# Softplus of a scan kernel as one table function over four tiles, and two subtractions moved from GpSimd to VectorE

## The chip, the cores and the metric

One Trainium2 chip, one of its cores. The metric is the device time of one execution in microseconds (us), the median of several runs. PE is TensorE, DVE is VectorE, ACT is ScalarE, POOL is GpSimd, SP is the engine that issues nearly all DMAs.

## The reference, cut to what matters

Four layers, each a state-space mixer over a batch of 64 images of 11 x 11 positions and 128 channels, then a feed-forward part (mixture of experts, two recurrent ones, one with spectral filters). The change lies in the mixer, which is the same in all four layers, with other weights. Per layer:

```python
xz = x @ in_proj_w.T
xc, z = split(xz, 2)                          # 256 channels each
xc = silu(conv1d(xc as (B, 256, 121), 3 taps) + conv_b)
t = xc.transpose(0, 2, 1)                     # 121 "channels" d, 256 places l
# for each of two directions k, from t:
dts, Bs, Cs = x_proj_w[k] applied to t        # 8, 16, 16 rows
delta = softplus(dt_proj_w[k] @ dts + dt_proj_b[k])
dA  = exp(delta[..., None] * A)               # 16 states n
dBu = delta[..., None] * Bs * t[..., None]
h   = scan over l of  h = dA * h + dBu
y_k = sum_n h * Cs + Ds[k] * t
y = y_0 + flip(y_1);  normalized, times gelu(z), projected back to 128 channels
```

All values are fp32. `dts` and `dt_proj_w` are folded into one matrix `w_dt` (121 x 121 and a bias row), so that the argument of Softplus is one matmul of `t`.

## The kernel before, in words

**Stages.** Each layer is a scan stage of some 1630 to 1645 us from its first to its last scan (`Conv.run`, L771) and a feed-forward stage. The batch of 64 is cut into eight chunks c of CB = 8 images. A chunk has two directions k, so there are 16 *sets* (c, k), numbered m = 2c + k. A set has 121 channels d, taken two at a time: 61 *steps* (`PAIRS`), so a chunk has 122 steps and a layer 976. The partitions of the scan are 16 states x 8 images = 128.

**One scan step g** (two channels, 512 columns):
- `rows` (L677): TensorE spreads delta's rows, stored in three bf16 parts that add up to the fp32 value, over the 128 partitions into `da` in PSUM, a ring of five buffers. It is issued three steps ahead.
- `exps` (L690): ScalarE takes the exponential in place, with the scale A of its channel, two instructions, also three steps ahead.
- `load_u` (L654): SP loads `ub`, delta times t for four channels (two steps), 512 KB, from DRAM, spread over the states. Seven buffers, issued 14 steps ahead; SP waits there until the buffer's old scans are done.
- `times_b` (L666): GpSimd multiplies `ub` by B in place, 1024 columns, issued five steps ahead.
- `scan` (L698): VectorE scans `da` (PSUM) and `ub` (SBUF) into `H` or `HX`.
- `by_c` (L719) on TensorE sums over the states, and `keep_y` collects the sums: a copy on ScalarE for k = 0 (L736), an addition on VectorE for k = 1 (L734).

**Work laid beside the scans.** While chunk c is scanned, the next chunk's inputs are made: `lead` (normalization, transposes, the convolution, Silu, L264), `steps` (delta, below), `aside` (B and C, and the term with Ds: `scaled` on ScalarE, L393, then `skip` on VectorE, L398); and the chunk before is finished: `tail`, whose `scales2` (two small functions on ScalarE, L187 and L188) is followed a step later by `scales3` on VectorE (L192). `gate` makes Gelu (L433). The place of each piece is written out by hand: `at(step, f)` puts a function into a dictionary by step, `lay` spreads a list over a range of steps, `lay_at` takes (step, function) pairs; `run` emits for each step the rows and exponentials of g + 3, the loads and products that are due, the scan, and then that step's pieces. Every engine runs its instructions in this order, and an instruction that waits holds up all behind it on its engine.

**Delta (`steps`, L283).** A set has four *tiles* of two images, 128 x 512. The set (0, 0) is made before any scan starts (`alone`), with scratch space in `H`; the other 15 sets of a layer lie beside scans. Each tile goes through:

1. `project` (L304): TensorE, the argument x into PSUM (`p`).
2. `parts` (L311): ScalarE, relu(x) and |x| into SBUF.
3. `e` (L314, L319): ScalarE, p = exp(-|x|), then w = p + 1 (when alone, the addition is VectorE's, L317).
4. `ln` (L323): ScalarE, ln(w).
5. `less` (L326), `delta` (L329, L330): VectorE, relu(x) + (ln(w) - ((w - 1) - p)). Each reads one operand from PSUM and one from SBUF.
6. `first` (L335): ScalarE, the first bf16 part, into `d[:, 0]`; `u` (L339): GpSimd, delta times t; `rest` (L343): GpSimd, delta less the first part; `second` (L346): ScalarE, the second part; `third` (L350): GpSimd, what is left, as bf16. When alone, `rest` and `third` are VectorE's.
7. `store` (L353, L354): two DMAs on SP, `d` to `dD` and `u` to `uD` in DRAM, from where `load_r` and `load_u` fetch them. `d` and `u` have two buffers each.

With start s, tile i begins at s + i * apart; its operations 1 to 5 and `first` follow one step apart, then `u` at 6 + late, `rest` at 7 + late, `second` at 8.5 + late, `third` at 8 + 2 late, `store` at 10 + 2 late. For chunks from the third on, in steps of the chunk beside which they lie: k = 0 starts at 49, k = 1 at 95, both with apart 11.6 and late 6.

**Tables.** ScalarE's functions come in table sets. `act_tables(nc, 6)` (L69) loads the set with the exponential and the logarithm; a load in front of a function that isn't in the loaded set is put there when the kernel is built. Silu and Gelu stand each between two loads.

## Time and profile before

| what | us |
|---|---|
| median of three runs (lowest, highest) | 8470.6 (8464.77, 8479.49) |
| profiled execution, from its first to its last instruction (the span) | 8458.2 |
| scan stages, first to last scan, four layers | 1644.7, 1638.9, 1642.5, 1628.9 |
| a steady chunk (layer 0, third), span | 208.3 |
| VectorE busy in it | 178.3 |
| GpSimd busy in it | 182.6 |
| ScalarE busy in it | 169.3 |

The profile is of one execution; of its time only the span is given. A group line gives source line, engine, operation, written tile and read tiles, shape, count, then total busy us, the mean ns of one, and after the second bar the engine's idle time just before these instructions with what ended it. A line of a timeline gives start, duration, engine, line, operation, tiles, and in brackets the idle time before it. A line of waits gives who waited for whom: total us, times, longest. Delta's own groups beside the scans, all 128 x 512 and 240 times, with mean ns: ScalarE L311 590 and 598, L314 593, L319 688, L323 627, L335 611, L346 609; VectorE L326 682, L329 682, L330 687; GpSimd L339 1280, L343 1163, L350 1161. At the start of a layer, on VectorE, L343 680 and L350 1105.

### The profile page before, as it was taken

Reading aid. Unit: us, or ns where it says so; the run is one execution under the profiler, and the core shown is the slowest. Engines: PE = TensorE matmul, PEld = TensorE weight load, DVE = VectorE, ACT = ScalarE, POOL = GpSimd, SP = SyncE. Lnnn points to the kernel's source line nnn. Section 1 sums busy time; section 2 is a strip of 40 time slices with the busy share of each in tenths; the row PEclk is TensorE's granted clock in tenths of the full one; section 3 lists DMA queues with packets and bytes.
Section 4 is the critical chain, followed back from the end, with each engine's and each line's share of the span. In section 5 each row is a group of like instructions: output and inputs, shape, how many; then the busy total and the mean of one; then the engine's idle time right before and its main releaser. Section 6 shows DMA issues by size and latency. Waiting matters only on the chain.

```text
span 8458.2 us, 209204 instructions
## 1 busy us (share of the span) xinstructions
PE 5994.4 (71%) x83374; PEld 3445.8 (41%) x83374; DVE 6141.0 (73%) x8636; ACT 5768.7 (68%) x12927; POOL 5832.5 (69%) x3139
## 2 busy tenths in 40 slices
PE   5676677676677767767677777666567776766999
PEld 3343343355344434344344444344333433433445
DVE  6888888854888888872788888882688888883211
ACT  6888888743888878862788788863688888873210
POOL 6888888921988888850888888870688888890000
PEclk7777777767777777776777777766777778778999
DMA  6888998946898899960899999981689888992111
GB/s 171 221 224 223 223 226 225 232 140 177 218 224 225 224 220 222 230 181 25 222 220 227 221 226 226 224 205 31 179 226 225 230 225 226 226 231 72 39 34 37
DMA packets 933130, 1603.70 MB, mean 190 GB/s; under 512 B 139912, under 2 KB 620514, under 8 KB 932151
## 3 DMA queue, kind: packets, MB, share of 16 engines
q1 hardware_dynamic: 930871, 1588.21, 74.6%
q8 instruction: 655, 10.73, 0.6%
q14 instruction: 324, 2.65, 0.1%
q10 hardware_dynamic: 1280, 2.10, 0.1%
HBM read 1299.53 MB, written 290.52 MB: 188 GB/s over the span
## 4 chain that ended last, share of the span: by engine, by line
PE 31%; ACT 20%; DMA 17%; DVE 14%; issue 8%; POOL 7%; SPq 1%; DVEq 0%; POOLq 0%; ACTq 0%
ACT da L690 7%; DVE H L698 5%; DMA ub<-uD 5%; POOL ub L666 5%; PE da L677 4%; PE yb L719 4%; PE pc L253 4%; DVE HX L698 3%; DMA ts<-sD 3%; PE pu L1306 3%; PE acc L1309 3%; PE out L1349 2%; DMA uD<-u 2%; PE pst L1193 2%; DMA R<-dD 2%
## 5 line engine op out<-in xcount | busy, mean ns | idle before, releaser
L666 POOL TENSOR_TENSOR ub<-ub,Bt 128x1024 f32<-128x1024 f32 (+1 forms) x1984 | 4564.0, 2317 | 731.8 <-DMA ub<-uD 526.1
L690 ACT ACTIVATE da<-da,A 128x255 f32<-128x255 f32 x7744 | 3389.6, 446 | 1094.7 <-PE da L677 918.7
L698 DVE TENSOR_TENSOR_SCAN H<-da,ub 128x512 f32<-128x512 f32 x2048 | 2391.8, 1205 | 93.6 <-POOL ub L666 42.0
L677 PE MATMUL da<-R,pick 120*128 120x255 bf16 x7744 | 1783.5, 324 | 938.0 <-DVE H L698 529.4
L698 DVE TENSOR_TENSOR_SCAN HX<-da,ub 128x512 f32<-128x512 f32 (+1 forms) x1856 | 2115.6, 1187 | 90.5 <-issue 52.4
L677 PEld LDWEIGHTS <-pick 120*128 120x128 bf16 x7744 | 599.6, 104 | 1638.3 <-issue 777.1
L719 PE MATMUL yb<-H,Cz 128*16 128x64 f32 x32768 | 867.6, 255 | 349.8 <-ACT yst L736 260.4
L719 PE MATMUL yb<-HX,Cz 128*16 128x64 f32 x32768 | 856.5, 246 | 209.9 <-ACT yst L736 102.5
L719 PEld LDWEIGHTS yb<-H,Cz 128*16 128x16 f32 x32768 | 604.5, 112 | 921.4 <-issue 520.1
L719 PEld LDWEIGHTS yb<-HX,Cz 128*16 128x16 f32 x32768 | 562.4, 110 | 680.7 <-issue 316.8
L734 DVE TENSOR_TENSOR yst<-yst,yb 128x512 f32<-128x512 f32 (+2 forms) x640 | 340.2, 548 | 272.7 <-PE yb L719 272.5
L253 PE MATMUL pc<-w_conv,xnT 128*121 128x256 f32 x1344 | 441.6, 426 | 55.2 <-ACT t L257 55.1
L174 POOL MEMSET t<- 128x2048 f32 x4 | 7.2, 1804 | 597.4 <-PE px L1200 416.3
L736 ACT COPY yst<-yb 128x512 f32<-128x512 f32 (+2 forms) x640 | 330.6, 543 | 109.3 <-DMA yD<-yst 43.1
L304 PE MATMUL pd<-t,w_dt 122*128 122x512 f32 x480 | 358.3, 839 | 54.6 <-ACT t L264 54.6
L339 POOL TENSOR_TENSOR u<-relu,t 128x512 f32<-128x512 f32 x240 | 307.2, 1280 | 22.7 <-DVE relu L330 22.6
L350 POOL TENSOR_TENSOR d<-relu,d 128x512 bf16<-128x512 f32 x240 | 278.6, 1161 | 54.1 <-ACT d L346 53.9
L1273 DVE COPY U<-pu 128x488 f32<-128x488 f32 x128 | 85.4, 667 | 283.4 <-PE pu L1306 283.4
L1275 ACT COPY U<-pu 128x488 f32<-128x488 f32 x128 | 72.9, 569 | 309.2 <-PE pu L1306 309.2
L343 POOL TENSOR_TENSOR relu<-relu,d 128x512 f32<-128x512 f32 x240 | 279.1, 1163 | 6.6
L253 PEld LDWEIGHTS pc<-w_conv,xnT 128*121 128x121 f32 x1344 | 233.7, 209 | 102.8 <-ACT t L257 81.6
L643 POOL TENSOR_TENSOR Cz<-Cp,own 128x512 f32<-128x512 f32 x256 | 274.4, 1072 | 0.0
(242 smaller groups left out, 7929.8 us busy)
## 6 DMA issues: line engine op xcount, KB each, us to landing
ub<-uD SPq DMA_DIRECT2D x1920, 512.0 KB
dD<-d SPq DMA_DIRECT2D x256, 384.0 KB
R<-dD SPq DMA_DIRECT2D x192, 420.0 KB
uD<-u SPq DMA_DIRECT2D x256, 256.0 KB
sD<-s SPq DMA_DIRECT2D x128, 256.0 KB
yD<-yst SPq DMA_DIRECT2D x512, 60.5 KB
ts<-sD SPq DMA_DIRECT2D x56, 512.0 KB
y<-yD SPq DMA_DIRECT2D x112, 242.0 KB
```

The source lines that it names most:

```text
L253: nc.tensor.matmul(pc, lhs, rhs, start=(j == 0), stop=(j == taps - 1))
L304: nc.tensor.matmul(s["p"], self.w_dt[:, k, :], tb[: D + 1], start=True, stop=True)
L339: nc.gpsimd.tensor_mul(s["u"], s["relu"], tb)
L343: less.tensor_sub(s["relu"], s["relu"], s["d"][:, 0, :])
L350: less.tensor_sub(s["d"][:, 2, :], s["relu"], s["d"][:, 1, :])
L666: self.nc.gpsimd.tensor_mul(x, x, self.bc[m, "Bt"].unsqueeze(1).to_broadcast([128, n, L]))
L677: self.nc.tensor.matmul(self.da[g % RING][:, j, 1:], self.pick[:n, d % 5].rearrange("p n b -> p (n b)"), self.R[m, d // 35][:n, d % 35 // ...
L690: self.nc.scalar.activation(x, x, AF.Exp, scale=self.A[:, m % 2, d : d + 1])
L698: self.nc.vector.tensor_tensor_scan(self.H[dq % 2][:, :n, p - DQ[dq][0]], self.da[g % RING].rearrange("p j l -> p (j l)")[:, :n], x.rearra ...
L719: self.nc.tensor.matmul(self.yb[32 * q : 32 * q + 16, slot % 8, :, :, :w], self.Cz[slot // 8][:, place % 64 : place % 64 + 2, :].rearrange ...
L734: nc.vector.tensor_add(dst, dst, src)
L736: nc.scalar.copy(dst, src)
```

## The change

Softplus becomes one table function. Beside the scans, ScalarE copies each of the four projections from PSUM into a 2048-column buffer `sp`; then one instruction takes Softplus of all four tiles in place, with a table load ahead of it (put there when the kernel is built) and an explicit load of set 6 behind it. `parts`, `e`, `ln`, `less` and `delta` are gone. In the set made alone, Softplus reads each projection from PSUM by itself, and set 6 is loaded once behind the last tile; the load of set 6 behind the first chunk's Silu is left out. `rest` and `third` are VectorE's everywhere; both operands of each are in SBUF. The constants of the plan change: from the third chunk on, k = 0 has its projections at steps 49, 51, 53, 55, each copied a step later, Softplus at 57, and tile i begins at 58 + 8.3 i with `u` and `first`; k = 1 has Softplus at 103 and tiles at 104 + 11.6 i. `rest`, `second`, `third`, `store` follow at late, late + 2, late + 4, late + 6. For the second chunk (laid beside the first) k = 0 has Softplus at 75, tiles 6 apart, late 4, and k = 1 starts at 103 with tiles 9.3 apart; the set (0, 1) has Softplus at 8, tiles 8 apart, late 3.

```diff
-        self.one = fixed.tile([128, 1], F32, name="one")
-        nc.vector.memset(self.one, 1.0)
...
-            if b1 == CB:
+            if b1 == CB and c > 0:
                 act_tables(nc, 6)
...
         alone = c == 0 and k == 0
+        v = {}
+
+        def soft():
+            nc.scalar.activation(v["sp"], v["sp"], AF.Softplus)
+            act_tables(nc, 6)
+
         for b in range(0, CB, 2):
...
-            def parts(s=s, tile=tile):
-                for n, f in (("relu", AF.Relu), ("abs", AF.Abs)):
-                    s[n] = tile(n)
-                    nc.scalar.activation(s[n], s["p"], f)
-
-            def e(s=s, tile=tile):
-                nc.scalar.activation(s["p"], s["abs"], AF.Exp, scale=-1.0)
-                s["w"] = tile("w")
+            def keep(b=b, s=s):
                 if alone:
-                    nc.vector.tensor_scalar_add(s["w"], s["p"], 1.0)
-                else:
-                    nc.scalar.activation(s["w"], s["p"], AF.Identity, bias=self.one)
-
-            def ln(s=s, tile=tile):
-                s["ln"] = tile("ln")
-                nc.scalar.activation(s["ln"], s["w"], AF.Ln)
-
-            def less(s=s):
-                nc.vector.scalar_tensor_tensor(s["p"], s["w"], -1.0, s["p"], ALU.add, ALU.subtract)
-
-            def delta(s=s):
-                nc.vector.tensor_sub(s["p"], s["ln"], s["p"])
-                nc.vector.tensor_add(s["relu"], s["relu"], s["p"])
-
+                    s["sp"] = self.spare[0][:, 256 * b : 256 * b + 512]
+                    nc.scalar.activation(s["sp"], s["p"], AF.Softplus)
+                    if b == CB - 2:
+                        act_tables(nc, 6)
+                    return
+                if b == 0:
+                    v["sp"] = work.tile([128, CB // 2 * 512], F32, name="sp", bufs=1)
+                s["sp"] = v["sp"][:, 256 * b : 256 * b + 512]
+                nc.scalar.copy(s["sp"], s["p"])
...
-                nc.scalar.copy(s["d"][:, 0, :], s["relu"])
+                nc.scalar.copy(s["d"][:, 0, :], s["sp"])
...
-                nc.gpsimd.tensor_mul(s["u"], s["relu"], tb)
+                nc.gpsimd.tensor_mul(s["u"], s["sp"], tb)
 
             def rest(s=s):
-                less = nc.vector if alone else nc.gpsimd
-                less.tensor_sub(s["relu"], s["relu"], s["d"][:, 0, :])
+                nc.vector.tensor_sub(s["sp"], s["sp"], s["d"][:, 0, :])
 
             def second(s=s):
-                nc.scalar.copy(s["d"][:, 1, :], s["relu"])
+                nc.scalar.copy(s["d"][:, 1, :], s["sp"])
 
             def third(s=s):
-                less = nc.vector if alone else nc.gpsimd
-                less.tensor_sub(s["d"][:, 2, :], s["relu"], s["d"][:, 1, :])
+                nc.vector.tensor_sub(s["d"][:, 2, :], s["sp"], s["d"][:, 1, :])
...
-            at = start + b // 2 * apart
-            for i, f in enumerate((project, parts, e, ln, less, delta, first)):
-                out.append((at + i, f))
-            at += 6
-            for i, f in ((late, u), (late + 1, rest), (late + 2.5, second), (2 * late + 2, third), (2 * late + 4, store)):
-                out.append((at + i, f))
+            if alone:
+                at = start + b // 2 * apart
+                out += [(at, project), (at + 1, keep)]
+                at += 2
+            else:
+                out += [(start + b, project), (start + b + 1, keep)]
+                at = start + CB + 1 + b // 2 * apart
+            offsets = (0, 0, 0, 1, 1, 2) if alone else (0, 0, late, late + 2, late + 4, late + 6)
+            out += [(at + i, f) for i, f in zip(offsets, (u, first, rest, second, third, store))]
+        if not alone:
+            out.append((start + CB, soft))
         return sorted(out, key=lambda x: x[0])
...
-        self.lay_at(self.steps(0, 1, 0, 8.5, 2))
+        self.lay_at(self.steps(0, 1, 0, 8, 3))
...
-                a, b, e, apart, late, f = (24, 42, 66, 8.3, 2, 101) if c == 0 else (0, 16, 48, 11.6, 6, 95)
+                a, b, e, apart, late, f = (24, 42, 66, 6, 4, 103) if c == 0 else (0, 16, 48, 8.3, 6, 95)
...
-                self.lay_at(self.steps(c + 1, 1, s + f, (139 - f) / 4 if c == 0 else 11.6, late))
+                self.lay_at(self.steps(c + 1, 1, s + f, 9.3 if c == 0 else 11.6, late))
```

More of the change, by code (lines that the diff above doesn't have):

```diff
@@ L290, in steps @@
             tb = self.t[:, b : b + 2, :].rearrange("p b l -> p (b l)")
-            def tile(n, b=b):
-                if alone:
-                    at = 1024 * b + 512 * ("relu", "abs", "w", "ln").index(n)
-                    return self.spare[0][:, at : at + 512]
-                tag, bufs = ("abs", 1) if n == "ln" else (n, 2 if n == "relu" else 1)
-                return work.tile([128, 512], F32, name=n, tag=tag, bufs=bufs)
             def project(b=b, s=s, tb=tb):
```

## The prediction

> **What bounds the kernel now.** I read the page's busy line, then stretches of one steady chunk (layer 0, third chunk, scan steps 70 to 105), then who waits on VectorE, then single instructions.
>
> ```profile
> PE 5994.4 (71%) x83374; PEld 3445.8 (41%) x83374; DVE 6141.0 (73%) x8636; ACT 5768.7 (68%) x12927; POOL 5832.5 (69%) x3139
> ...
> L666 POOL TENSOR_TENSOR ub<-ub,Bt 128x1024 f32<-128x1024 f32 (+1 forms) x1984 | 4564.0, 2317 | 731.8 <-DMA ub<-uD 526.1
> L690 ACT ACTIVATE da<-da,A 128x255 f32<-128x255 f32 x7744 | 3389.6, 446 | 1094.7 <-PE da L677 918.7
> L698 DVE TENSOR_TENSOR_SCAN H<-da,ub 128x512 f32<-128x512 f32 x2048 | 2391.8, 1205 | 93.6 <-POOL ub L666 42.0
> ```
>
> The shares of 68 to 73% are averages over four scan stages (about 6550 us) and four feed-forward stages. By stretch (VectorE is the third busy column, GpSimd the fifth, then clock, DMA share, GB/s):
>
> ```profile
> 548.60:587.00 38.40, 30.77 (x465) 18.41 (x464) 27.66 (x41) 28.86 (x63) 31.06 (x14) 0.83 1.01 266
> 587.00:618.90 31.90, 23.71 (x388) 15.96 (x389) 28.68 (x38) 28.72 (x69) 24.69 (x16) 0.62 0.79 176
> 618.90:684.80 65.90, 46.61 (x804) 23.78 (x805) 61.49 (x74) 55.40 (x127) 65.74 (x36) 0.79 0.89 238
> ```
>
> From 618.9 to 684.8 us, GpSimd is full (65.7 of 65.9), VectorE nearly so (61.5). Steps 30 to 50 (548.6 to 587.0) belong to the DMA (share 1.01). So no engine alone is the bound, and freeing GpSimd helps only as far as VectorE, the next in line, lets it. VectorE runs the scans in order, and every stall of it is a stall of the chain. In this chunk of 208.3 us it is busy 178.3 and idle 30. What its idle time waits for:
>
> ```profile
> DVE yst L734 <- PE yb L719: 272.5, 175, 4.8
> ...
> DVE pd L326 <- ACT w L319: 104.4, 95, 2.9
> DVE tr L192 <- ACT tr L188: 92.3, 34, 3.6
> DVE pd L329 <- ACT ln L323: 91.7, 72, 4.6
> ```
>
> GpSimd is hardly among its releasers (42 us at L698). So I cost the change on VectorE's time line.
>
> **What the skill says.** First, the Trainium skill, "SBUF — State Buffer", section "Who interferes with whom": a VectorE instruction with two SBUF inputs takes the port pair that it shares with GpSimd, and is shut out for as long as a GpSimd instruction reading SBUF runs, and the reverse; with one SBUF input it isn't. The trace agrees, in both directions, at the start of layer 0, where the two subtractions already run on VectorE:
>
> ```profile
> 49.20 0.68 DVE L343 TENSOR_TENSOR H<-H,d 128x512 f32<-128x512 f32 x1
> 49.43 1.61 POOL L339 TENSOR_TENSOR u<-H,t 128x512 f32<-128x512 f32 x1 [2.50 <-DVE H L330]
> ...
> 57.09 1.29 POOL L339 TENSOR_TENSOR u<-H,t 128x512 f32<-128x512 f32 x1 [6.05 <-DMA uD<-u]
> 57.39 1.53 DVE L350 TENSOR_TENSOR d<-H,d 128x512 bf16<-128x512 f32 x1 [1.48 <-ACT d L346]
> 58.85 0.68 DVE L343 TENSOR_TENSOR H<-H,d 128x512 f32<-128x512 f32 x1
> ```
>
> GpSimd's product takes 1.61 us instead of 1.29 behind a subtraction; the subtraction that finds it running takes 1.53 instead of 0.68: it ends 0.54 after the product (58.38). All other VectorE work around the scans, the scans too, has at most one input in SBUF. Second, "ScalarE: Activation LUTs", section "What ACT_TABLE_LOAD costs": 1283 ns a load, plus some 1380 of drain. The trace has the 1.28, but the next function starts at once (below), so I count no drain. Third, same page, "Step-by-step: what each stage is for": 0.833 ns an element whatever the function; here gelu over 1936 columns took 1.82 us (L433), so Softplus over 2048 is taken as 1.9.
>
> **The change, part by part.** A layer has 16 delta sets of four tiles; one runs alone before the scans. That leaves 60 sets, 240 tiles in the kernel. VectorE instructions of 0.69 us follow each other every 0.60 (48.60, 49.20, 49.81 at the start), so 0.60 is what one takes of the line.
>
> (1) Three VectorE operations per tile go (L326, L329, L330): 720 x 0.60 = -432 us.
>
> (2) Their waits for ScalarE go: 104.4 + 91.7 = -196 us. What is late next: the scan behind them, whose inputs were there (it waited 20 us for da).
>
> (3) Two subtractions per tile come: 480 x 0.60 = +288 us. The operations read at most one buffer that ScalarE wrote two steps (3.4 us) before, and u's product stands four or six steps ahead; no further wait.
>
> (4) The shared port. GpSimd was busy 182.6 of 208.3 us in the chunk; without 8 tiles x 2 x 1.16 (L343, L350) it is 164, so with a chunk of about 213 a subtraction finds it busy 0.77 of the time. What then remains of its instruction is half of it: half of 2.37 for the products with B (88% of its time), half of 1.1 to 1.3 for the rest, together 1.11; the example shows that 0.13 of that is covered by VectorE's own start. So 0.77 x 0.98 = 0.76 us each, 480 x 0.76 = +365 us. Queued behind it on VectorE is the next scan; TensorE's rows (a ring of five) and the loads of ub wait for that scan. Bounds: 0 (always finds it idle) and 0.98 each, 470 us.
>
> (5) Softplus between two loads: 1.28 + 1.9 + 1.28 = 4.5 us of ScalarE in one piece, 60 times. The nearest thing is the Silu block, with scales2 a step later:
>
> ```profile
> 580.94 1.28 ACT L264 ACT_TABLE_LOAD   x1
> 582.23 2.00 ACT L264 ACTIVATE t<-t 121x1024 f32<-121x1024 f32 x2
> 584.25 1.28 ACT L71 ACT_TABLE_LOAD   x1
> ...
> 586.93 0.16 DVE L192 SCALAR_TENSOR_TENSOR tr<-pk,tr 128x4 f32<-128x4 f32 x1 [3.65 <-ACT tr L188]
> ```
>
> Of 4.6 us of block, VectorE lost 3.65, although exponentials run three steps ahead. The new block at step 57 has the same neighbour: the tail's scales2 at 58 and scales3 on VectorE at 59. That at 103 has `scaled` at 103 and `skip` on VectorE at 104. In six chunks of each layer both occur: 48 x 3.65 = 175; the other 12 blocks have no such neighbour, 0.75 each: together +184 us. Bounds: 0 (the lead hides it) and 60 x 4.6 = 276.
>
> (6) The set before the scans, where everything waits for it: from the last Silu (37.40) to the last store (66.55) the kernel spends 29 us. New: load 38.7, Softplus 39.3, u 40.7 (rest overwrites what u reads), rest, second, third, store by 43.5; the next tiles follow some 3.5 us apart, each held by its d buffer's earlier store (2.9 us from 53.28 to 56.22), last store near 55. -11 us a layer, -44 us.
>
> (7) TensorE: the fourth projection (L304) of a set stood at step 83 amid the projections for B and C, where VectorE waited 3 us for yb (part of the 272.5). It moves to step 55, where TensorE has room: 24 x 1.3 = -30 us.
>
> (8) At nothing: ScalarE loses 743 us (relu 142, abs 144, exp 142, identity 165, ln 151) and gains 240 copies x 0.57 and 60 x 4.5, net -336, but isn't the bound; GpSimd's 558 us relief (some 180 given back to the port) likewise, since VectorE hardly waited for it. Stores (both DMAs of `store`, on SP's queue, with the loads of ub behind) move from steps 71 to 106 to 70 to 95, and by one step for k=1; nothing new waits there. The two d and u buffers come free 4.6 steps (7.7 us) after a store's issue; if that is late, ScalarE and GpSimd wait up to 2 us, with lead to cover it; without it, 24 x 2 tiles x 1 = 50 us.
>
> Sum: -432 - 196 + 288 + 365 + 184 - 44 - 30 = +135 us. The span 8458.2 becomes 8593; the median of 8470.6 stands 12.4 above the span (the page gives no other time), which I keep: 8606 us.
>
> **Rivals.** *A, the forecast*: VectorE is the line, the port decides; +135, own range 8500 to 8820. *B, faster*: VectorE comes to its subtraction when GpSimd has just finished. Where GpSimd sets the pace, a pair of scans (2.4) ends as a product (2.37) ends, so what remains would be near zero; with VectorE the pace-maker GpSimd stands waiting for ub loads (already 526 us). At 0.25 us each, (4) is 120, the sum -110: 8360. It decides below 0.76 - 135/480 = 0.48 us. For it: in stretch 548.6 to 587.0 GpSimd waits. Against: no subtraction falls in that stretch; they fall at steps 64 to 93 and 110 to 149. *C, no change*: the port wait is near 0.48, or half the blocks hide: 8470. *D, much slower*: GpSimd's instructions follow without a gap, and if a waiting subtraction isn't let in between, it waits for a further product: + 480 x 2.37 = 1138, 9740. No row shows VectorE waiting with a second product queued. *E, the edit does not do what it says*: if copies brought loads of their own, 240 x 1.28 on ScalarE; the copies beside Silu and Gelu show none.
>
> **How the numbers follow.** A 0.58, B 0.26, C 0.07, D 0.09, E negligible. About 0.2% (17 us) is what a measurement tells from no change here. Faster 0.26, same 0.07, slower 0.58 + 0.09 = 0.67. The range reaches up to (4) and (5) at their upper bounds: 135 + 105 + 92 + 20 = +352, 8825; down to the middle of B, 8375; left out are B's lower half and most of D.
>
> **What would show it.** (1), (2): L326 and L329 gone from VectorE's waits. (4): the subtractions on VectorE with a mean near 0.68 + 0.76 = 1.4 us; a mean under 1.1 means B, over 2.5 D. GpSimd's products grow slightly over 2.37. (5): ScalarE with 120 more table loads; VectorE's wait L192 for L188 about doubled, and a new one of `skip` for `scaled`. (6): the first scan 11 us earlier. I am wrong if the steady chunk isn't longer than 208 us although the subtractions take 1.4.

## The result, and the profile after

| | kernel before | changed kernel |
|---|---|---|
| median of four runs, us (lowest, highest) | 8467.69 (8464.61, 8479.49) | 8566.44 (8558.9, 8570.5) |
| span of the profiled execution, us | 8458.2 | 8561.2 |
| granted TensorE clock, mean | 0.778 | 0.77 |

The ratio is 1.0116, 95% interval 1.0102 to 1.0131: the change costs 98.8 us. The forecast was 8606 us, with 8500 to 8820 as the likeliest case's own range.

The page of the changed kernel, its busy line and the groups that the prediction spoke of (line, engine, operation, tiles and shape, count, then busy us, mean ns, and the idle time before with what ended it; lines are those of the changed kernel, 15 to 20 lower than before: L321 is `u`, L324 `rest`, L330 `third`, L651 the products, L675 the exponentials, L683 the scans):

```profile
PE 6088.2 (71%) x83374; PEld 3490.2 (41%) x83374; DVE 6254.9 (73%) x8328; ACT 5526.0 (65%) x12103; POOL 5460.7 (64%) x2659
...
L651 POOL TENSOR_TENSOR ub<-ub,Bt 128x1024 f32<-128x1024 f32 (+1 forms) x1984 | 4664.3, 2371 | 839.4 <-DMA ub<-uD 664.7
L675 ACT ACTIVATE da<-da,A 128x255 f32<-128x255 f32 x7744 | 3393.5, 446 | 1329.4 <-PE da L662 1160.0
L683 DVE TENSOR_TENSOR_SCAN H<-da,ub 128x512 f32<-128x512 f32 x2048 | 2392.0, 1205 | 111.5 <-POOL ub L651 61.0
...
L321 POOL TENSOR_TENSOR u<-sp,t 128x512 f32<-128x512 f32 x240 | 319.3, 1330 | 487.6 <-ACT sp L289 419.3
...
L324 DVE TENSOR_TENSOR sp<-sp,d 128x512 f32<-128x512 f32 x240 | 371.6, 1548 | 0.0
L330 DVE TENSOR_TENSOR d<-sp,d 128x512 bf16<-128x512 f32 x240 | 294.2, 1226 | 0.0
```

VectorE has 308 instructions fewer (8328 for 8636) and is busy 114 us longer. ScalarE and GpSimd are relieved, by 243 and 372 us, and the kernel is slower all the same. The two subtractions (L324, L330) take 1.55 and 1.23 us where the same shapes took 1.16 on GpSimd. The exponentials and the products wait more, for the rows and the loads. Rows and loads wait in turn for a buffer that a scan of VectorE has to free (rows for scans: 1003 us, 690 before), so I take these waits for a consequence, not for the cause.

By stretches, the third chunk of layer 0 again (steps 30 to 50, 50 to 70, 70 to 105; columns as in the prediction):

```profile
549.72:587.30 37.58, 31.35 (x464) 18.74 (x462) 27.61 (x42) 28.50 (x62) 29.71 (x14) 0.77 1.05 265
587.30:622.39 35.09, 24.56 (x449) 15.71 (x448) 27.61 (x34) 32.17 (x71) 24.77 (x14) 0.80 0.73 170
622.39:687.84 65.45, 42.08 (x684) 21.94 (x683) 58.00 (x65) 45.11 (x97) 54.76 (x28) 0.78 0.86 234
```

The prediction's third window, 618.9 to 684.8 us, is not steps 70 to 105, as it says: the scan of step 105 began at 677.98, and the window runs on to step 109. The same steps before:

```profile
618.94:677.98 59.04, 41.02 (x716) 21.57 (x715) 54.63 (x68) 49.66 (x115) 58.88 (x33) 0.78 0.87 235
```

The stretch bound by the DMA (share 1.05) is as long as before (37.6 for 38.4 us). The second, which now holds a Softplus block (step 57), is 3.2 us longer than before, with VectorE busy no longer than it was (27.6 for 28.7). The third is 6.4 us longer: VectorE is busy 3.4 us longer (58.0 for 54.6) and idle 3.0 us longer, and it is now the fullest engine, while GpSimd, full before (58.9 of 59.0), has gaps. Steps 0 to 30, where four projections, their functions and the waits behind them are gone, took 53.2 and now 46.9. The whole chunk: 208.3 before, 212.6 after.

The same over all layers, mean length of each chunk in us, from its first scan to the next chunk's, for the eighth to the end of its last scan:

| chunk | 1st | 2nd | 3rd | 4th | 5th | 6th | 7th | 8th |
|---|---|---|---|---|---|---|---|---|
| before | 205.7 | 207.0 | 208.9 | 209.7 | 208.4 | 209.4 | 208.6 | 181.7 |
| after | 219.6 | 214.8 | 214.5 | 212.3 | 211.8 | 212.0 | 211.4 | 176.6 |

Over the four layers the first chunks give +55 us, the second to seventh +99, the eighth, beside which no delta is made, -20, and the start of the layers -43: from the last Silu to the first scan it takes 31 to 33 us instead of 42 to 43 (in layer 0 the first scan begins at 69.58 us instead of 79.76). That is +91; the spans differ by 103, and the other 12 us lie between a layer's last scan and the next layer's last Silu, mostly in the feed-forward stages, which the change doesn't touch.

What VectorE waits for in the changed kernel (total us, times, longest):

```profile
DVE tr L190 <- ACT tr L186: 197.5, 59, 4.5
DVE yst L719 <- PE yb L704: 191.5, 127, 4.9
DVE y L453 <- PE pk L445: 166.1, 45, 6.9
...
DVE s L383 <- ACT ps L378: 118.5, 32, 6.2
...
DVE y L453 <- DMA y<-yD: 44.8, 12, 5.9
```

and in the kernel before, for two of them:

```profile
DVE y L468 <- PE pk L460: 48.1, 10, 6.3
...
DVE s L398 <- ACT ps L393: 5.8, 25, 1.4
```

The waits for Softplus's steps (196 us before) are gone. `scales3` for `scales2` (L190) went from 92.3 to 197.5, `skip` for `scaled` (L383) from 5.8 to 118.5, the tail's normalization for its transposes (L453 for pk) from 48.1 to 166.1; the wait for yb fell from 272.5 to 191.5, that for y's load from 90.5 to 44.8. In sum VectorE's idle time is 11 us less than before: nearly all that was saved in waits was given back in other waits. With 114 us more of busy time, that is the difference of the spans, 103 us.

The two mechanisms can be seen in single instructions. The port, beside the third chunk of layer 0 (start, duration, engine, line, operation; VectorE first, then GpSimd):

```profile
626.39 2.23 DVE L324 TENSOR_TENSOR sp<-sp,d 128x512 f32<-128x512 f32 x1
...
633.59 2.84 DVE L330 TENSOR_TENSOR d<-sp,d 128x512 bf16<-128x512 f32 x1
...
628.03 1.51 POOL L628 TENSOR_TENSOR Cz<-Cp,own 128x512 f32<-128x512 f32 x1
...
633.52 2.36 POOL L651 TENSOR_TENSOR ub<-ub,Bt 128x1024 f32<-128x1024 f32 x1
635.82 1.53 POOL L628 TENSOR_TENSOR Cz<-Cp,own 128x512 f32<-128x512 f32 x1
```

The second subtraction starts just behind a product (633.52 to 635.88) and takes 2.84 us: it ends at 636.43, 0.55 after the product. GpSimd's next instruction takes 1.53 instead of its usual 1.07 (the one at 628.03, behind the first subtraction, 1.51): it waits for the subtraction in turn, and so the subtraction was let in between two instructions that follow each other without a gap. So it was with all that waited: 317 of the 480 found GpSimd in the way, each ended 0.55 us after the GpSimd instruction that was then running, and behind 287 of them GpSimd's next one followed within 0.2 us. The longest of all 480 is 2.88 us. This is what the Trainium skill says in "SBUF — State Buffer", "Who interferes with whom": whichever starts first keeps the pair for its whole instruction, and the other one waits. Who comes next when GpSimd has a further instruction ready, the page doesn't say; the last section shows that being let in is not certain.

The block, at step 57 of the second chunk of layer 0, ScalarE:

```profile
390.06 1.28 ACT L289 ACT_TABLE_LOAD   x1
391.35 1.91 ACT L289 ACTIVATE sp<-sp 128x2048 f32<-128x2048 f32 x1
393.28 1.28 ACT L71 ACT_TABLE_LOAD   x1
394.58 0.93 ACT L675 ACTIVATE da<-da,A 128x255 f32<-128x255 f32 x2
```

For 4.5 us no exponential is taken. Beside it VectorE waits 4.46 us in front of L190, and GpSimd, whose product `u` (L321) stands right behind Softplus, waits 7.85:

```profile
396.47 0.16 DVE L190 SCALAR_TENSOR_TENSOR tr<-pk,tr 128x4 f32<-128x4 f32 x1 [4.46 <-ACT tr L186]
...
393.34 1.26 POOL L321 TENSOR_TENSOR u<-sp,t 128x512 f32<-128x512 f32 x1 [7.85 <-ACT sp L289]
```

### The profile page after: what moved, and what is told of

Read it like the earlier page. It is cut to its first block, busy times and chain, and to the rows that moved or that the text cites. A ratio compares the mean times of both kernels' runs of the same rounds, so it can differ in the third digit from the quotient of the medians.

```text
span 8561.2 us, 207075 instructions
## 1 busy us (share of the span) xinstructions
PE 6088.2 (71%) x83374; PEld 3490.2 (41%) x83374; DVE 6254.9 (73%) x8328; ACT 5526.0 (65%) x12103; POOL 5460.7 (64%) x2659
## 4 chain that ended last, share of the span: by engine, by line
PE 35%; ACT 20%; DVE 18%; DMA 13%; issue 9%; POOL 3%; SPq 1%; DVEq 0%; ACTq 0%; POOLq 0%
ACT da L675 7%; DVE H L683 7%; PE da L662 6%; PE yb L704 5%; DVE HX L683 4%; PE pc L251 4%; DMA ts<-sD 3%; DMA ub<-uD 3%; PE pd L301 3%; PE acc L1294 2%; PE out L1334 2%; PE pu L1291 2%; POOL ub L651 2%; PE pst L1178 2%; DMA bcD<-bc 2%
## 5 line engine op out<-in xcount | busy, mean ns | idle before, releaser
L651 POOL TENSOR_TENSOR ub<-ub,Bt 128x1024 f32<-128x1024 f32 (+1 forms) x1984 | 4664.3, 2371 | 839.4 <-DMA ub<-uD 664.7
L675 ACT ACTIVATE da<-da,A 128x255 f32<-128x255 f32 x7744 | 3393.5, 446 | 1329.4 <-PE da L662 1160.0
L683 DVE TENSOR_TENSOR_SCAN H<-da,ub 128x512 f32<-128x512 f32 x2048 | 2392.0, 1205 | 111.5 <-POOL ub L651 61.0
L683 DVE TENSOR_TENSOR_SCAN HX<-da,ub 128x512 f32<-128x512 f32 (+1 forms) x1856 | 2119.9, 1185 | 67.1 <-POOL Cz L628 19.0
L662 PEld LDWEIGHTS <-pick 120*128 120x128 bf16 x7744 | 624.6, 104 | 1738.0 <-issue 1199.0
L321 POOL TENSOR_TENSOR u<-sp,t 128x512 f32<-128x512 f32 x240 | 319.3, 1330 | 487.6 <-ACT sp L289 419.3
L301 PE MATMUL pd<-t,w_dt 122*128 122x512 f32 x480 | 323.3, 760 | 247.6 <-ACT sp L313 194.6
L719 DVE TENSOR_TENSOR yst<-yst,yb 128x512 f32<-128x512 f32 (+2 forms) x640 | 337.9, 544 | 192.9 <-PE yb L704 191.5
L324 DVE TENSOR_TENSOR sp<-sp,d 128x512 f32<-128x512 f32 x240 | 371.6, 1548 | 0.0
L499 PE MATMUL po<-out_wT,y 128*121 128x128 f32 x896 | 202.6, 366 | 154.1 <-DVE tr L190 103.8
L628 POOL TENSOR_TENSOR Cz<-Cp,own 128x512 f32<-128x512 f32 x256 | 306.9, 1199 | 0.0
L330 DVE TENSOR_TENSOR d<-sp,d 128x512 bf16<-128x512 f32 x240 | 294.2, 1226 | 0.0
```

The costliest lines, as they stand in the source:

```text
L301: nc.tensor.matmul(s["p"], self.w_dt[:, k, :], tb[: D + 1], start=True, stop=True)
L321: nc.gpsimd.tensor_mul(s["u"], s["sp"], tb)
L324: nc.vector.tensor_sub(s["sp"], s["sp"], s["d"][:, 0, :])
L628: self.nc.gpsimd.tensor_mul(self.Cz[u], C.unsqueeze(2).to_broadcast([128, 64, CB]), self.own.unsqueeze(1).to_broadcast([128, 64, CB]),)
L651: self.nc.gpsimd.tensor_mul(x, x, self.bc[m, "Bt"].unsqueeze(1).to_broadcast([128, n, L]))
L662: self.nc.tensor.matmul(self.da[g % RING][:, j, 1:], self.pick[:n, d % 5].rearrange("p n b -> p (n b)"), self.R[m, d // 35][:n, d % 35 // ...
```

## The experiments

Two accounts of the +98.8 us stood against each other. The *port account*: the subtractions beside GpSimd's products cost what decides. The *block account*: Softplus between its loads does. Each ratio below is to the kernel before, run on the same chip. The changed kernel was not run again beside them: its own ratio, to compare, is 1.0116 (1.0102 to 1.0131), and where a time of it is needed, it is 1.0116 times the kernel before on that chip, an estimate good to some 12 us.

### The subtractions back on GpSimd

```diff
-                nc.vector.tensor_sub(s["sp"], s["sp"], s["d"][:, 0, :])
+                less = nc.vector if alone else nc.gpsimd
+                less.tensor_sub(s["sp"], s["sp"], s["d"][:, 0, :])
```

and the same for `third`.

> The changed kernel with the two subtractions beside the scans back on GpSimd; Softplus as one function stays. Port theory: the subtractions cost VectorE 480 x (0.60 + 0.71) = 630 us of its line, so VectorE is relieved by that, GpSimd takes 558 us back and becomes the bound in the stretches where it was full before: 8350 to 8450 us, GpSimd idle in a steady chunk back to about 25 us, VectorE idle up to 40. Block theory (the 4.5 us pieces of ScalarE make the change slower, and the port waits fall into time that VectorE would have idled): within 30 us of the changed kernel, 8540 to 8600.

Measured: 8428.21 us, ratio 0.9981 (0.9971 to 0.999). Moving the 480 subtractions from VectorE to GpSimd turns a loss of 1.2% into a gain of 0.2%, as the port account expected (8350 to 8450 us): their place is enough to decide the sign. This run doesn't tell the port from the instructions themselves. And the gain is small for an engine that got 595 us of work less:

```profile
PE 6062.8 (72%) x83374; PEld 3458.4 (41%) x83374; DVE 5659.5 (67%) x7848; ACT 5494.7 (65%) x12103; POOL 5813.9 (69%) x3139
```

```profile
DVE yst L721 <- PE yb L706: 380.9, 201, 8.4
...
DVE HX L685 <- ACT da L677: 99.8, 75, 2.6
DVE HX L685 <- POOL ub L653: 95.4, 95, 3.3
DVE H L685 <- POOL ub L653: 87.5, 50, 14.9
```

VectorE's busy time falls from 6255 to 5660 us, and its idle time grows by 454: it now waits for TensorE's sums (381 for 192), and for exponentials and products (in the order of the lines 100, 95 and 87 us, for 18, 3 and 61 in the changed kernel). With the subtractions gone, VectorE is not the only bound any more.

### The old Softplus with the subtractions on VectorE

The kernel before, with only this edit:

```diff
-                less = nc.vector if alone else nc.gpsimd
+                less = nc.vector
```

in `rest` and in `third`.

> The kernel before with the two subtractions moved to VectorE, and nothing else of the change. Port theory: + 480 x (0.60 + 0.71) = 630 us on VectorE's line, a part of it back where GpSimd had been full: 8800 to 9050 us, mean of a subtraction 1.3 to 1.5 us. Block theory: 8440 to 8500, since GpSimd's relief pays for VectorE's load.

Measured: 8828.04 us, ratio 1.0457 (1.0437 to 1.0476), +384 us, inside the port account's range; the mean of the 480, 1.54 us, lies just above it. The two groups of this kernel:

```profile
L343 DVE TENSOR_TENSOR relu<-relu,d 128x512 f32<-128x512 f32 x240 | 405.7, 1690 | 2.6 <-POOL u L339 2.6
...
L350 DVE TENSOR_TENSOR d<-relu,d 128x512 bf16<-128x512 f32 x240 | 331.9, 1383 | 15.7 <-ACT d L346 15.7
```

The move alone costs 384 us; VectorE is busy 680 us longer, and its idle time falls by 312. Made in the kernel with the new Softplus, the same move costs 113 us (8428.21 to 1.0116 x 8443.6 = 8541.5). So the two edits don't add up. In the kernel before, more than half of the 680 us that VectorE got came out as time; in the kernel with the new Softplus, where VectorE is busy 595 us longer with the subtractions, a fifth did. There its idle time shrank by 454 us to take them in, for 312 here.

### The same VectorE instructions without the port

Beside the scans, an instruction with one SBUF input of the same size takes the place of each subtraction. The subtractions are left out, so the three parts no longer add up to delta:

```diff
-                nc.vector.tensor_sub(s["sp"], s["sp"], s["d"][:, 0, :])
+                if alone:
+                    nc.vector.tensor_sub(s["sp"], s["sp"], s["d"][:, 0, :])
+                else:
+                    nc.vector.reduce_max(s["sp"], s["sp"].unsqueeze(2), axis=AX.X)
```

and likewise for `third`.

> The changed kernel in which beside the scans each of the two subtractions is replaced by a maximum over one element, an instruction of VectorE of the same size with a single SBUF input; the subtraction is left out (the parts of delta no longer add up). Port theory: the mean of these 480 instructions falls from 1.39 to about 0.7 us, 330 us less on VectorE's line, time 8230 to 8330 us. Block theory: the time stays within 40 us of the changed kernel.

Measured: 8276.03 us, ratio 0.9805 (0.9783 to 0.9828). Its groups:

```profile
L327 DVE TENSOR_REDUCE sp<-sp 128x512 f32<-128x512 f32 x240 | 158.4, 660 | 0.0
L336 DVE TENSOR_REDUCE d<-sp 128x512 bf16<-128x512 f32 x240 | 158.5, 660 | 0.0
```

All 480 take 653 to 680 ns, beside the same products. VectorE is busy 338 us less than in the changed kernel, GpSimd 170 less, and the time is 265 us less (8541.5 to 8276.0). The instructions themselves aren't the price; what they wait for is. The edit also takes away that each subtraction needs ScalarE's copy just before it, but there was nothing to gain there: in the changed kernel VectorE's idle time in front of L324 and L330 is 0.0.

### Softplus without its loads

A function that is in set 6 takes the place of Softplus, which is left out, and the explicit load goes:

```diff
-            nc.scalar.activation(v["sp"], v["sp"], AF.Softplus)
-            act_tables(nc, 6)
+            nc.scalar.activation(v["sp"], v["sp"], AF.Exp)
```

> The changed kernel with an exponential in place of Softplus beside the scans and so without the 120 table loads: the block on ScalarE is 1.9 us instead of 4.5; Softplus is left out. Port theory: the 48 blocks with a neighbour that VectorE waits for lose 2.6 us each, 48 x 2.6 = 125 us: 8430 to 8480. Block theory: the whole of the loss and more comes back, 8330 to 8400.

Measured: 8315.0 us, ratio 0.9844 (0.9822 to 0.9866): 226 us less than the changed kernel, for 154 us less of ScalarE (120 loads of 1.283 us). The function took the same 1.91 us. So the loads cost 3.8 us of time a block for 2.6 us of ScalarE. The port account expected far less (8430 to 8480 us), and even the block account, nearer, less than this (8330 to 8400); of the two, this run speaks for the block. VectorE's waits in it:

```profile
DVE yst L718 <- PE yb L703: 145.7, 131, 5.3
DVE tr L190 <- ACT tr L186: 132.7, 62, 3.6
DVE y L452 <- PE pk L444: 132.7, 34, 6.0
```

The wait of L190 falls from 197.5 to 132.7, that of `skip` from 118.5 to 32.3, yb from 191.5 to 145.7, pk from 166.1 to 132.7. VectorE is busy as long as in the changed kernel (6251 for 6255): the 226 us are all waits. Little of it can come by way of GpSimd's `u`, whose wait for Softplus fell from 419 to 331 us only.

Both accounts are true, then: port 265, loads 226. They need not add, and no run takes both away.

### The blocks away from their neighbours

If the block costs because `scales3` and `skip` stand behind it, it should cost less elsewhere. From the third chunk on, two steps later for k = 0 and five for k = 1, whose tiles stand 11 apart for 11.6:

```diff
-                self.lay_at(self.steps(c + 1, 0, s + e + 1, apart, late))
-                self.lay_at(self.steps(c + 1, 1, s + f, 9.3 if c == 0 else 11.6, late))
+                self.lay_at(self.steps(c + 1, 0, s + e + (1 if c == 0 else 3), apart, late))
+                self.lay_at(self.steps(c + 1, 1, s + f + (0 if c == 0 else 5), 9.3 if c == 0 else 11, late))
```

> The changed kernel with the Softplus blocks of the third and later chunks moved away from the ScalarE instructions that VectorE waits for: k = 0 two steps later (Softplus at 59, behind scales2 at 58), k = 1 five steps later (at 108, behind the last `scaled` at 106), k = 1's tiles 11 apart. Theory of neighbours: the cost is in what stands right behind the block (scales3's and skip's waits, 105 and 103 us more than before, and TensorE's work held up behind them); 150 to 220 us come back, ratio to the kernel before 0.985 to 0.995. Theory of ScalarE's time: 4.5 us without an exponential starve the scans wherever they stand; at most 60 us come back, ratio 1.004 to 1.012, with new waits of the scans for da.

Measured: 8575.17 us, ratio 1.0151 (1.0132 to 1.0171): no gain, rather a loss. It lies outside what either account expected (0.985 to 0.995 for the neighbours, 1.004 to 1.012 for ScalarE's time). The neighbours' waits did fall (L190 from 197 to 141, `skip` from 118 to 28), but the scans themselves began to wait in their place:

```profile
DVE H L683 <- POOL u L321: 92.8, 24, 3.9
```

and the subtractions, which now met other instructions of GpSimd, took 1.49 us in the mean instead of 1.39. That is 48 us of VectorE, under which a small gain could lie hidden: this run alone doesn't decide. The same move with the subtractions on GpSimd, where VectorE doesn't wait for the port, tells more: it brought 0.9974 for 0.9981 (below), in a kernel in which GpSimd is fuller. My account by neighbours falls.

### The second chunk's tiles farther apart

The first chunk of a layer, beside which the second chunk's delta is made, lost most (+13.9 us), and in that of layer 0 GpSimd waited 10.9 us and ScalarE 7.3 us for the stores out of the two `u` and `d` buffers.

```diff
-                a, b, e, apart, late, f = (24, 42, 66, 6, 4, 103) if c == 0 else (0, 16, 48, 8.3, 6, 95)
+                a, b, e, apart, late, f = (24, 42, 66, 7, 3, 103) if c == 0 else (0, 16, 48, 8.3, 6, 95)
```

> The changed kernel with other constants for the second chunk's sets alone, which lie beside the first: tiles 7 apart and late 3 instead of 6 and 4, so that the two d and u buffers have five steps instead of two from a store's issue to their next use. Theory of the buffers: the 8.9 us (GpSimd, u) and 6.9 us (ScalarE, d) of waits for stores in steps 90 to 100 of the first chunk cost about 6 us of each layer, so 20 to 30 us come back. Rival: the first chunk is longer by 14 us because of the blocks alone; within 17 us of the changed kernel.

Measured: 8536.6 us, ratio 1.0111 (1.0086 to 1.0137), not to be told from 1.0116; the first chunk took 221.5 us in the mean (219.6 before the edit). The waits for those stores halved over the kernel (`u` from 83 to 40 us, `first` from 69 to 35), and no time came of it. So it isn't shown that the buffers make the first chunk long. It remained long in other runs too (214.8 with the one-input instructions, 217.1 without the loads, 217.1 with the subtractions on GpSimd), so neither the port alone nor the loads alone explain it. Its cause stays open.

### GpSimd's product farther from Softplus

```diff
-            offsets = (0, 0, 0, 1, 1, 2) if alone else (0, 0, late, late + 2, late + 4, late + 6)
+            offsets = (0, 0, 0, 1, 1, 2) if alone else (late - 2, 0, late, late + 2, late + 4, late + 6)
```

> The changed kernel with GpSimd's product u two steps ahead of `rest` instead of at the tile's first step, where it stands behind Softplus (GpSimd waits 419 us for it). Theory that GpSimd isn't the line: that wait vanishes, GpSimd waits for ub loads instead, time within 25 us of the changed kernel. Rival (GpSimd's products, queued behind u, make the scans late): 60 to 150 us come back.

Measured: 8503.81 us, ratio 1.0065 (1.0044 to 1.0086), so 43 us less than the changed kernel, between the two expectations (within 25; 60 to 150). GpSimd's wait for Softplus fell from 419 to 33 us. Its wait for loads, 664.7 us in the changed kernel, has grown instead:

```profile
POOL ub L651 <- DMA ub<-uD: 934.1, 567, 14.9
```

Most of the 419 us only changed its name, from waiting for Softplus to waiting for loads. A tenth of it was time. How it came is not shown: the scans' wait for products is as it was (63 for 61 us); the subtractions took 1.35 us in the mean instead of 1.39, and VectorE's waits for yb and pk were 147 and 137 us for 191 and 166.

### Both together, and a look at what the block does

The moved blocks with `u` later, that is, the diff of the blocks and the last one together. It tells whether moving failed only because `u` then stood in front of products that a scan needed.

> The changed kernel with both: the blocks moved away from scales3 and skip, and u two steps ahead of `rest`. Moving alone took 113 us of VectorE's waits away and gave 93 back as scans that wait for GpSimd's u, which waits for Softplus. Theory of the queue (every instruction placed right behind Softplus holds up its engine, on VectorE directly, on GpSimd by the products behind it): with both out of the way the gains add, ratio to the kernel before 0.990 to 0.999. Rival (the block starves the scans wherever it stands): no better than u later alone, 1.003 to 1.010.

Measured: 8547.45 us, ratio 1.0125 (1.0105 to 1.0145): worse than `u` later by itself (1.0065), and worse than either account expected (0.990 to 0.999; 1.003 to 1.010). Part of that is the port again, with subtractions of 1.46 us in the mean for 1.35; but VectorE's idle time is the same in both (2245 and 2249 us). The block costs no less in a place without neighbours. And the scans' wait that the profile puts down to `u` reads as in the run that moves the blocks, 92.8 us, 24 times, 3.9 at most, though `u` now stands four steps later. The trace shows why. ScalarE, then VectorE:

```profile
400.00 1.28 ACT L289 ACT_TABLE_LOAD   x1
401.30 1.91 ACT L289 ACTIVATE sp<-sp 128x2048 f32<-128x2048 f32 x1
403.23 1.28 ACT L71 ACT_TABLE_LOAD   x1
404.52 0.93 ACT L675 ACTIVATE da<-da,A 128x255 f32<-128x255 f32 x2
```

```profile
399.36 2.31 DVE L683 TENSOR_TENSOR_SCAN H<-da,ub 128x512 f32<-128x512 f32 x2
405.54 1.23 DVE L683 TENSOR_TENSOR_SCAN H<-da,ub 128x512 f32<-128x512 f32 x1 [3.86 <-POOL u L321]
407.59 1.23 DVE L683 TENSOR_TENSOR_SCAN H<-da,ub 128x512 f32<-128x512 f32 x1 [0.83 <-ACT da L675]
409.24 1.23 DVE L683 TENSOR_TENSOR_SCAN H<-da,ub 128x512 f32<-128x512 f32 x1 [0.42 <-POOL ub L651]
```

The block stands behind the exponentials of three further scans. But when it begins, at 400.00, the first of these scans is done and the second running: VectorE has 1.7 us of work left. Then it stands for 3.86 us: the profile names GpSimd's `u`, but that ended at 404.55, the product that this scan reads at 390.40, and what ended last were the exponentials behind the block (404.52 + 0.93 = 405.45). The next two scans wait again, 0.83 and 0.42 us, since the lead has to be built up anew. In this place a block of 4.5 us cost 5.1 us. Exponentials three steps ahead don't mean three scans in hand: of the three, less than one and a half were left.

### Towards a better version

The subtractions on GpSimd, with the moved blocks and the second chunk's tiles apart (three of the diffs above):

> Softplus as one function, the subtractions on GpSimd, the blocks moved as in the run that moves them, and the second chunk's tiles 7 apart: a candidate for better than both. Port theory with the theory of neighbours: ratio to the kernel before 0.975 to 0.988 (the 0.998 of the subtractions on GpSimd, less 100 to 200 us), GpSimd full from step 60 to 110. If ScalarE's time counts wherever the block stands: 0.994 to 1.000.

Measured: 8421.09 us, ratio 0.9974 (0.9965 to 0.9984), beside 0.9981 without the moves: nothing worth naming, and not the 0.975 to 0.988 that the account by neighbours asked for.

The same with `u` later as well, the fourth diff:

> The same two moves with the subtractions on GpSimd and the second chunk's tiles 7 apart. Theory of the queue: the 93 us of scans waiting for u go, ratio 0.983 to 0.992. Rival: 0.995 to 0.999, since GpSimd is full there.

Measured: 8360.84 us, ratio 0.9899 (0.9883 to 0.9916). This version beats both kernels, by 82 us the one before. The ratio is in the range expected (0.983 to 0.992), but not for the reason given there: the 93 us of scans that the profile puts down to `u` were to go, and they are still 97.2 us. With GpSimd as full as it is here (5825 us), the place of `u` counts for more than in the changed kernel: 60 us lie between this run and the one ahead of it, for 43 there. The version without the moved blocks was not run. What VectorE still waits for:

```profile
DVE yst L721 <- PE yb L706: 445.7, 190, 5.2
```

One subtraction on each engine (`rest` on VectorE, `third` on GpSimd), all moves kept:

```diff
-                nc.vector.tensor_sub(s["d"][:, 2, :], s["sp"], s["d"][:, 1, :])
+                less = nc.vector if alone else nc.gpsimd
+                less.tensor_sub(s["d"][:, 2, :], s["sp"], s["d"][:, 1, :])
```

> As the one with the subtractions on GpSimd and all moves, but `rest` on VectorE and `third` on GpSimd, a candidate for the best: half of the port's 340 us, half of GpSimd's 558. Port theory: between the two, 0.975 to 0.990, as neither engine is full; the 240 subtractions on VectorE about 1.5 us each, since GpSimd is busier. Rival: worse than both, over 1.0.

Measured: 8403.44 us, ratio 0.9957 (0.9942 to 0.9972). It is slower by 43 us than both on GpSimd, where the expectation was 0.975 to 0.990. The 240 that stay on VectorE took 1.86 us each, more than `rest` in any other run (1.75 in the same place with `third` on VectorE too).

A longer lead for the exponentials, four steps instead of three, on the best version:

```diff
-        for g in range(3):
+        for g in range(4):
...
-                if g + 3 < G:
-                    self.rows(g + 3)
-                    self.exps(g + 3)
+                if g + 4 < G:
+                    self.rows(g + 4)
+                    self.exps(g + 4)
```

> The best so far (subtractions on GpSimd, blocks moved, u later) with rows and exponentials issued four steps ahead instead of three, on the same ring of five. Theory that a block costs what the lead of the exponentials doesn't cover: one more scan (1.2 us) is covered at each of 60 blocks, at Silu's and Gelu's too: 70 to 130 us less, ratio 0.975 to 0.982. Rival: with the ring full, TensorE stands at rows(g + 4) until scan(g - 1) is done, and its sums yb behind it come later: no gain, 0.988 to 1.01, with more waits of VectorE for yb.

Measured: 8390.54 us, ratio 0.9936 (0.9919 to 0.9952), 31 us slower than with three, as the rival expected (0.988 to 1.01). In the waits of VectorE and of TensorE:

```profile
DVE yst L721 <- PE yb L706: 572.0, 310, 6.3
```

```profile
PE da L664 <- DVE H L685: 698.1, 652, 8.0
PE da L664 <- DVE HX L685: 404.5, 501, 7.6
```

TensorE's rows wait 1103 us for a buffer of the ring (663 with three steps), and behind them, in the same queue, stand the sums yb, for which VectorE then waits 572 instead of 446 us. With five buffers a lead of four brought nothing. More buffers weren't tried.

## Why the prediction was right or wrong

The sign was right, the size nearly (+135 for +98.8). The shared port, named as the first cause, is one of two of like size: it is worth 265 us (forecast 365) and the table loads alone 226 (the forecast for the whole blocks was 184). That the sum came so near is in part luck: the port's term was 100 us too large, the blocks' at least 42 too small, and 43 us of `u` were left out, which cancel for the most part. One step was mis-sized because it took all of a wait for time, one for a wrong reason, and one was wrong outright.

**(1), (2), right.** The three operations on VectorE (492 us of busy time) and both their waits (196 us) are gone. The bet that the scan behind them would not be late for other reasons held only in part: see (5) and (7).

**(3), (4), the wait right, its worth in time too large.** 480 subtractions of 1.387 us in the mean (forecast 1.44): 0.71 above the 0.68 of one alone, 340 us for 365. Both factors held within some 15%: at 400 of 480 starts GpSimd was busy (0.83, forecast 0.77), and 317 of these then waited 1.07 us in the mean, or 0.85 over the 400 (forecast 0.98). The instructions with one input showed that this is what costs, but that not all of it is time: 338 us less of VectorE, 265 us less of time. What was wrong is to count each microsecond of the wait as one of the kernel's. The first subtraction waits longer (1.55) than the second (1.23), where the forecast took them as equal: 182 of the first met GpSimd's work, 135 of the second. Why is not shown.

**(5), mis-sized for a wrong reason.** The forecast put 184 us on the 60 blocks whole, since each has `scales3` or `skip` close behind. Those two waits did grow by 105 and 113 us, 218 for the 175 foretold (4.5 us a block for the 3.65 of the one example). But the loads alone, which leave a 1.9 us function in place, cost 226 us, and moving the blocks from their neighbours gave nothing (1.0151, 1.0125 with `u` later, and 0.9974 for 0.9981 where no subtraction is on VectorE). So the neighbours are only where the loss shows: a block longer than the work in hand stops VectorE in both places that were tried.

**(6), right.** The first scan came 10.2 to 11.6 us earlier a layer, -43 us for -44; the last tile's stores were issued at 55.0 and 55.6 (forecast near 55).

**(7), half right.** VectorE's wait for yb fell by 81 us, more than the 30 foretold. What the step left out is where the four projections went. They stand two steps apart now and TensorE waits for ScalarE's copy to empty the PSUM tile (194.6 us, 151 times; before, none). The tail's transposes are in the same queue, and VectorE's wait for pk grew by 118 us. That the one caused the other is argued from the order of the queue, and is part of it at most: without the loads TensorE waited as long (196.6 us), and pk's wait was 132.7 for 166.1; with the subtractions on GpSimd it was 121.6.

**(8), wrong for `u`.** "At nothing" left out that a set's first `u` moved from seven steps behind its input (from the third chunk on) to right behind it: GpSimd waited 419 us for Softplus, and putting `u` later gave back 43 us here and 60 us in the version with the subtractions on GpSimd. For the relief of ScalarE and GpSimd the step was right: 243 and 372 us less busy, and no gain. (ScalarE's 336 were a sum of single instructions, which shrank by 354 us in all; they overlap on the engine, so that less of its busy time went.) The two `d` and `u` buffers, for which it allowed up to 50 us, did make engines wait (`u` 83.3 us for its stores, `first` 68.6; before 41.9 and 31.8), without a measured cost: the run that spread them halved these waits and moved nothing. The first chunks' +55 us stand unexplained.

**The rivals.** B (VectorE arrives when GpSimd has just finished) asked for a mean under 1.1, D (VectorE is not let in between two products) for one over 2.5: 1.39 excludes both for the mean. Singly, both occur: 81 subtractions began in the last 0.2 us of a GpSimd instruction and waited for nothing, as B has it; and what D feared, that a subtraction is not let in, happened to none of the changed kernel's, but to a few in other runs (last section). C asked for a wait near 0.48 or half the blocks hidden: 0.71 and 226 us exclude it. E falls too: 124 more loads, 60 in front of Softplus, 60 behind and 4 in the sets made alone.

**The sum.** With the measured sizes in place of (4) and (5): -432 - 196 + 288 - 44 - 30 + 265 + 226 = +77, beside 98.8 measured; the remainder, 22 us, is half of what `u` in (8) was worth, and no single term can be named for it. That assumes that the costs add up, and the two placements of the subtractions (+384 and +113 us) warn that they need not.

**Around the span.** The forecast kept 12.4 us between the span and the time. It is 1.9 (8563.08 for a span of 8561.2): the profiled execution of before, 8460 us by the same sum, was quicker than all four runs. The other 10.5 us were the distance from that execution to the median; since they put the sum on the median, the forecast stays the same.

## What to carry to other kernels

Before an elementwise step goes to VectorE, ask how many of its inputs lie in SBUF and what GpSimd does beside it: here, with two such inputs the price was its own 0.68 us and another 0.71 of waiting, with one no wait at all. A function that needs its own table set is a piece of load, function, load on an engine that works in order: hold its length (4.5 us) against the work that the next engine really has in hand (1.7 us in the place looked at, not the nominal three scans), and don't place its first reader right behind it (43 us here). And if a merged function frees the bound engine, leave the room to the bound: here Softplus as one function is worth 1.0% with the subtractions left on GpSimd, `u` moved back and the other two moves, and costs 1.2% with the subtractions on VectorE and `u` right behind it.

## What the runs showed of the hardware that was not expected

- The wait for the port depends on where the subtractions fall: the mean was 1.39 us in the changed kernel, 1.49 with the blocks moved, 1.54 with the old Softplus. GpSimd's whole load doesn't order these (busy 5461, 5459 and 5417 us). The longest in the changed kernel, 2.88 us, is one product of 2.36 and 0.5.
- Being let in is likely, not certain. In the eight runs with subtractions on VectorE, 2609 of them waited for GpSimd, and 2605 ended 0.54 to 0.56 us after the GpSimd instruction that they had met, whether or not another followed at once. The other four were passed over for as long as GpSimd had work without a gap: for a second product (5.1 us, with `rest` alone on VectorE), for seven instructions (11.7 us, with the blocks moved) and twice for eight (13.4 us, without the loads). One of the last two, VectorE and then the first and last that it waited for:

```profile
2055.06 13.39 DVE L323 TENSOR_TENSOR sp<-sp,d 128x512 f32<-128x512 f32 x1
...
2054.37 1.07 POOL L627 TENSOR_TENSOR Cz<-Cp,own 128x512 f32<-128x512 f32 x1
2055.40 4.64 POOL L650 TENSOR_TENSOR ub<-ub,Bt 128x1024 f32<-128x1024 f32 x2
...
2066.83 1.07 POOL L627 TENSOR_TENSOR Cz<-Cp,own 128x512 f32<-128x512 f32 x1
```

  It ended at 2068.45, 0.55 us after the last, behind which GpSimd had nothing to do. What sets these four apart, no run shows.
- GpSimd waits too: its product `u` took 1.33 us in the mean (1.28 with the subtractions on GpSimd), the products with B 2.37 instead of 2.32.
- The Trainium skill, "ScalarE: Activation LUTs", "What ACT_TABLE_LOAD costs", gives a switch 1283 ns and about 1380 of drain. All of the 120 new loads beside the scans took 1283 ns. A load in front of Softplus began 17 to 19 ns after the instruction before it, Softplus or the next function 11 to 12 ns after a load: here there was no drain on either side, and a switch of table cost 1.3 us.
- Softplus over 2048 columns took 1.911 us, Exp over the same 1.908.
